# q for four batches at once with two levels of seven products, k and v for all batches first

## The chip, the cores and the metric

The kernel runs on one core of a Trainium2 chip. Time is device microseconds of one execution. TensorE (PE) multiplies, VectorE (DVE), ScalarE (ACT) and GpSimd (POOL) work on elements, SyncE (SP) issues nearly all transfers. PE writes to PSUM, eight banks of 128 partitions x 512 f32 columns; DVE and ACT read PSUM, POOL reads only SBUF. All data are f32.

## The reference

One pre-norm block over x of 8 batches x 256 tokens x 512. Cut to what matters:

```python
x = x + attention(layernorm(x), w_qkv, w_o)
x = x + ffn(layernorm(x), weight, bias, centroids, assignments)

# attention: 32 heads, 8 key heads (kv), head size 128, G = 4 query heads per key head
q, k, v = split(h @ w_qkv)                       # w_qkv: 512 x (4096 + 1024 + 1024)
scores = q @ k.T / sqrt(128) - slope[head] * sqrt(distance), masked to the past
out = softmax(scores) @ v
out @ w_o                                        # 4096 x 512

# ffn: p = softmax(h @ centroids.T / 0.1) over 64 clusters; hits = p > 0.01
# h @ weight.T + bias, kept where the row has a hit and the column's cluster has one anywhere
```

The factor on the bias and the draw of x don't change the work.

## The kernel before

The kernel is written for a scheduler that keeps the order of the program: each engine executes its instructions as the Python code emits them, and waits only for data and for buffers. The order of the code is the schedule.

**Tiling.** Two batches (512 tokens) make a pair `p`; a pair and a key head make a group `g` (32 of them), and a group has two units, one per batch (`u`, 64 of them). Unit `u` computes the scores of four query heads against one key head over 256 tokens. The causal mask is cut into quarters of 64 tokens (`Q`), so that only 1280 of 2048 columns of scores are made: `scores` streams 2 x 384 columns and four small late blocks, which lie in two halves of the array.

**Seven products for eight.** `strassen` (line 146) splits each of the projections of q, k and v once into 2 x 2 blocks and forms the result from seven block products instead of eight, with sums of blocks as factors (`a_sums`, `b_sums`, lines 117 and 130). Products 1, 6, 7 and 4 add up in one PSUM bank, which ACT copies out after each of them; products 2 and 5, 3 sit in other banks, and DVE adds them to the copies. `project_out` (line 505) does the same with the output projection of one unit. A q product of a group is four matmuls of 256 columns (line 155), so a group has 28.

The sums of the weights are made anew for every pair: POOL makes those of w_q (`a_sums(gp, wq[g + 2], ...)`) and of w_o and w_k, DVE those of w_v and of x. k and v of a pair are projected between the units of the pair (`project_k`, `project_v`), those of the next pair ahead of it.

**One unit in the order of the loop** (line 724 on). `scores(u)`; `attend(u - 2, 0)`; POOL's late adds of the output (`flush_adds`, line 548) and `subtract_max(u - 1)`; then, between steps of q, k and v (`qq`, `e`): the maximum of unit u over keys (`over_keys`, line 412), the attention `av` of unit u - 2, the exps of u - 1, the FFN tile of that slot (`f`), the output projection of u - 2 (`w`), the sums over keys of u - 1 (`sum_old`) and `rows()`.

`rows` calls `over_quadrants` (line 426): PE transposes the row statistics, DVE reduces them and takes a reciprocal, SP stores 64 x 32 numbers to HBM and loads them back as a broadcast to 128 partitions, once for the maximum (line 450) and once for 1 / sum (line 448). POOL subtracts that maximum in the next unit (line 457), ACT takes the exp, DVE sums it, and the next `rows` needs this sum.

**Around the loop.** x is normalised by pairs and transposed on PE (`norm_tile`). The alibi bias is made once for each key head in the first pair, kept in HBM and reloaded. The FFN of a pair runs during the next pair; the last two pairs' tiles run at the end. After the loop the column selection is known and the output rows are chosen and stored.

Of the kernel before, what the change touches and what calls it, by code (L numbers as in the profile page):

```python
# [14 lines left out]
F32 = mybir.dt.float32  # L15
# [9 lines left out]
NCL = 64  # L25
P = 128
NC_H = H // P
PT_TOK = 2 * S
NPAIR = B // 2
TPP = PT_TOK // P  # L30
NT = B * S // P
EPS = 1e-5
# [3 lines left out]
X2_BUFS = 8  # L36
Q = P // 2
DQ = 5 * Q
# [7 lines left out]
def sqrt_distances():  # L46

    r = np.arange(P // 2)  # L50
    quarter = lambda *n: np.concatenate([r + i * (P // 2) for i in n])

    def block(k, q):
        k, q = k[:, None], q[None, :]
        return np.where(q >= k, np.sqrt(np.maximum(q - k, 0).astype(np.float32)), np.float32(MASKED))

    own = block(r, r)
    d = np.concatenate([block(quarter(0, 1), quarter(1, 3, 2)), np.concatenate([own, own]),
                        block(quarter(3, 2), quarter(3))], axis=1)
    return np.ascontiguousarray(d.astype(np.float32))  # L60


@with_exitstack
def block_kernel(
# [3 lines left out]
    w_qkv: bass.AP,  # L68
# [3 lines left out]
    centroids_t: bass.AP,  # L72
# [11 lines left out]
    wpool = ctx.enter_context(tc.tile_pool(name="w", bufs=1))  # L84
    work = ctx.enter_context(tc.tile_pool(name="work", bufs=1))
    small = ctx.enter_context(tc.tile_pool(name="small", bufs=4))
    dram = ctx.enter_context(tc.tile_pool(name="dram", bufs=4, space=bass.MemoryType.DRAM))
    p_acc = ctx.enter_context(tc.tile_pool(name="p_acc", bufs=3, space=PSUM))
    p_long = ctx.enter_context(tc.tile_pool(name="p_long", bufs=1, space=PSUM))
    p_sc = ctx.enter_context(tc.tile_pool(name="p_sc", bufs=2, space=PSUM))  # L90
    p_tp = ctx.enter_context(tc.tile_pool(name="p_tp", bufs=1, space=PSUM))


    x2_hbm = [dram.tile([PT_TOK, H], F32, tag=f"x2_hbm{p}", name=f"x2_hbm{p}", bufs=1) for p in range(NPAIR - 2)]
    y_hbm = [dram.tile([PT_TOK, H], F32, tag=f"y_hbm{p}", name=f"y_hbm{p}", bufs=1) for p in range(NPAIR - 2)]
    alibi_hbm = [dram.tile([P, G * DQ], F32, tag=f"al_hbm{kv}", name=f"al_hbm{kv}", bufs=1) for kv in range(NKV)]

    sub = ALU.subtract
    gp, ve = nc.gpsimd.tensor_tensor, nc.vector.tensor_tensor

    def a_side(raw, s1, s2, s4):

        return dict(A11=raw[0], A12=raw[1], A21=raw[2], A22=raw[3], S1=s1, S2=s2, S3=raw[2], S4=s4)

    def b_side(raw, t1, t2, t4):

        return dict(B11=raw[0], B12=raw[1], B21=raw[2], B22=raw[3], T1=t1, T2=t2, T3=raw[1], T4=t4)

    def a_sums(tt, a, which="S1 S2 S3 S4"):
        for s in which.split():
            if callable(a[s]):
                a[s] = a[s]()  # L120
            if s == "S1":
                tt(a["S1"], a["A21"], a["A22"], ALU.add)  # L122
            elif s == "S2":
                tt(a["S2"], a["S1"], a["A11"], sub)  # L124
            elif s == "S3":
                tt(a["S3"], a["A11"], a["A21"], sub)
            else:
                tt(a["S4"], a["A12"], a["S2"], sub)

    def b_sums(tt, b, which="T1 T2 T3 T4"):  # L130
        for s in which.split():
            if callable(b[s]):
                b[s] = b[s]()
            if s == "T1":
                tt(b["T1"], b["B12"], b["B11"], sub)
            elif s == "T2":
                tt(b["T2"], b["B22"], b["T1"], sub)
            elif s == "T3":
                tt(b["T3"], b["B22"], b["B12"], sub)
            else:  # L140
                tt(b["T4"], b["B21"], b["T2"], sub)
# [4 lines left out]
    def strassen(name, tag, a, b, pairs, c, n):  # L146
# [14 lines left out]
        def step(i):  # L161
            if i in (1, "5p") or i == 5 and 5 not in ps:
# [3 lines left out]
                if at == 5:  # L166
                    product(5, ps[5], True)
# [917 lines left out]
```

## Time and profile before

| what | value |
|---|---|
| median of 3 runs | 1392.85 us (1392.62 to 1394.12) |
| profiled execution, first to last instruction | 1390.6 us |
| what lies around it in the median run | 2.25 us |
| PE busy, matmuls recorded | 1379.6 us (99%), 6391 |
| DVE busy | 934.6 us (67%) |
| POOL busy | 957.5 us (69%) |
| ACT busy | 379.7 us (27%) |
| mean granted TensorE clock | 0.999 |
| transfers | 194.54 MB, mean 140 GB/s |

How to read it: busy time is a union over an engine's instructions and says nothing by itself of what the end waits for. Matmuls are pipelined, and their recorded lengths overlap, so what one costs is read from the chain of waits, where each row holds only the time up to the next. A row of a group gives line, engine, operation, tiles written and read, shapes and count, then busy time and mean ns of one, then the engine's idle time before it and who ended it.

### The profile page before, as it was taken

How to read it: one execution, taken by the hardware profiler on the slowest of the kernel's cores; microseconds unless marked ns; L12 is line 12 of the kernel's file. 1: busy time of each engine (PE TensorE's matmuls, PEld its weight loads, DVE VectorE, ACT ScalarE, POOL GpSimd, SP SyncE). 2: the span in 40 equal slices, each digit the busy share in tenths (PEclk: the TensorE clock that was granted, in tenths of full speed). 3: DMA queues.
4: the chain of work that ended last, by engine and by line, in shares of the span. 5: the costliest groups of instructions: out<-in, count | busy, mean ns of one | idle time of the engine just before them, and what ended most of it. 6: DMA issues, size and time to landing. Idle time of an engine off the chain costs nothing.

```text
span 1390.6 us, 18165 instructions
## 1 busy us (share of the span) xinstructions
PE 1379.6 (99%) x6391; PEld 1082.7 (78%) x6391; DVE 934.6 (67%) x1852; ACT 379.7 (27%) x776; POOL 957.5 (69%) x1049
## 2 busy tenths in 40 slices
PE   9999999999999999999999999999999999999998
PEld 7777877877877778777878787877787778778775
DVE  5567756786556665768666767576766686666876
ACT  3322223422232212332213322233222122212332
POOL 6477757787575765768757577576867777577673
PEclk9999999999999999999999999999999999999999
DMA  5436343344242544423334435354414352424344
GB/s 200 138 98 206 108 151 130 138 156 141 95 175 80 183 162 150 168 101 142 118 123 146 132 131 186 125 171 156 141 61 156 111 194 103 156 87 149 138 154 137
DMA packets 88041, 194.54 MB, mean 140 GB/s; under 512 B 11824, under 2 KB 20784, under 8 KB 87952
## 3 DMA queue, kind: packets, MB, share of 16 engines
q1 hardware_dynamic: 86800, 191.52, 39.7%
q10 hardware_dynamic: 1104, 1.70, 0.5%
q8 instruction: 52, 0.85, 0.2%
q14 instruction: 37, 0.30, 0.1%
q0 software_dynamic: 48, 0.16, 0.0%
HBM read 179.21 MB, written 14.16 MB: 139 GB/s over the span
## 4 chain that ended last, share of the span: by engine, by line
PE 92%; DVE 5%; DMA 1%; POOL 1%; issue 1%; ACT 0%; SPq 0%; DVEq 0%; POOLq 0%; ACTq 0%
PE ps_oa L519 15%; PE ps_qa L155 15%; PE av L478 10%; PE ps_qc L155 8%; PE ps_oc L519 7%; PE sc L401 6%; PE sc_late L408 4%; PE ps_va L155 4%; PE ps_ka L155 4%; PE ps_ob L519 4%; PE ps_qb L155 3%; PE ps_f L565 2%; PE ps_kc L155 2%; PE ps_vc L155 2%; PE ps_lg L565 2%; PE ps_vb L155 1%
## 5 line engine op out<-in xcount | busy, mean ns | idle before, releaser
L551 POOL TENSOR_TENSOR x<-x,snap 128x256 f32<-128x256 f32 x189 | 136.5, 739 | 198.0 <-DVE x L545 134.6
L457 POOL TENSOR_TENSOR s<-s,bc 128x768 f32<-128x768 f32 x64 | 116.6, 1822 | 135.1 <-DMA bc<-row_hbm 135.1
L415 DVE TRANSPOSE_TENSOR_REDUCE r<-s 128x40 f32<-128x1280 f32 x128 | 192.6, 1505 | 10.2 <-ACT s L823 7.3
L478 PE MATMUL av<-s,v 64*128 64x256 f32 (+2 forms) x640 | 170.8, 442 | 0.0
L171 ACT COPY qT<-ps_qa 128x512 f32<-128x512 f32 x128 | 74.8, 584 | 320.5 <-PE ps_qa L155 320.5
L534 ACT COPY snap<-ps_oa 128x256 f32<-128x256 f32 x189 | 70.4, 373 | 271.8 <-PE ps_oa L519 271.8
L478 PEld LDWEIGHTS av<-s,v 128*128 128x128 f32 (+1 forms) x640 | 91.3, 188 | 61.8 <-issue 55.8
L519 PE MATMUL ps_oa<-wo,oT 128*128 128x256 f32 x512 | 132.2, 381 | 0.8 <-DVE oT L500 0.8
L155 PE MATMUL ps_qa<-xT,wq 128*128 128x256 f32 x512 | 124.2, 385 | 0.0
L155 PEld LDWEIGHTS ps_qa<-xT,wq 128*128 128x128 f32 x512 | 94.4, 190 | 21.8 <-issue 10.2
L519 PEld LDWEIGHTS ps_oa<-wo,oT 128*128 128x128 f32 x512 | 91.8, 190 | 17.5 <-DVE oT L500 2.4
L462 POOL TENSOR_TENSOR s<-s,bc 64x256 f32<-64x256 f32 (+1 forms) x128 | 96.8, 757 | 9.8
L401 PE MATMUL sc<-qT,kT 128*128 128x384 f32 x256 | 93.1, 486 | 0.0
L421 DVE TENSOR_TENSOR r<-r 64x8 f32<-64x8 f32 x128 | 82.2, 642 | 1.7
L403 DVE SCALAR_TENSOR_TENSOR s<-sc,alibi 128x384 f32<-128x384 f32 x128 | 69.7, 555 | 18.0 <-PE sc L401 14.0
L545 DVE TENSOR_TENSOR x<-x,ps_oc 128x256 f32<-128x256 f32 x128 | 53.4, 418 | 28.3 <-PE ps_oc L519 27.4
L122 POOL TENSOR_TENSOR o_s<-oT 128x256 f32<-128x256 f32 x64 | 48.1, 752 | 34.3 <-DVE oT L495 34.1
L408 PE MATMUL sc_late<-qT,kT 128*64 128x256 f32 x512 | 69.4, 392 | 0.0
L420 DVE TENSOR_TENSOR r<-r 128x8 f32<-128x8 f32 x128 | 65.2, 509 | 4.4
L519 PE MATMUL ps_oa<-wo_t,o_s 128*128 128x256 f32 x256 | 65.8, 379 | 0.7 <-POOL o_s L124 0.7
L495 DVE TENSOR_TENSOR oT<-av,bc 128x512 f32<-128x512 f32 x64 | 44.2, 690 | 32.9 <-DMA bc<-row_hbm 17.6
L519 PE MATMUL ps_oa<-wo_t,oT 128*128 128x256 f32 x256 | 65.8, 379 | 0.0
(207 smaller groups left out, 2952.1 us busy)
## 6 DMA issues: line engine op xcount, KB each, us to landing
bc<-row_hbm SPq DMA_DIRECT2D x128, 512.0 KB, 4.9
wq<-in_w_qkv SPq DMA_DIRECT2D x32, 1024.0 KB, 7.8
wo<-in_w_o SPq DMA_DIRECT2D x32, 1024.0 KB, 8.0
alibi<-al_hbm SPq DMA_DIRECT2D x24, 640.0 KB, 8.8
wv<-in_w_qkv SPq DMA_DIRECT2D x8, 1024.0 KB, 11.5
wk<-in_w_qkv SPq DMA_DIRECT2D x15, 512.0 KB, 9.7
al_hbm<-alibi SPq DMA_DIRECT2D x8, 640.0 KB, 9.0
x<-in_x SPq DMA_DIRECT2D x16, 256.0 KB, 9.6
```

Source lines behind the costliest of these rows:

```text
L155: nc.tensor.matmul(bank[:, cols], lhsT=lhsT, rhs=rhs, start=first and j == 0, stop=j == len(mms) - 1, skip_group_check=True)
L171: nc.scalar.copy(x, like(ps[1], x))
L401: nc.tensor.matmul(sc, lhsT=kT[:, quarters(t0, 0, 2)], rhs=qT[:, 2 * i : 2 * i + 2, quarters(t0, 1, 3)], start=True, stop=True)
L408: nc.tensor.matmul(sc[ts(half, Q), ts(k // 2, G * Q)], lhsT=kT[:, quarters(t0, key, 1)], rhs=qT[:, :, quarters(t0, query, 1)], start=k < 2 ...
L415: nc.vector.tensor_reduce(a, s.rearrange("p (j q) -> p j q", q=32), AX.X, op, apply_transpose=True)
L421: nc.vector.tensor_tensor(first[Q:, :, 2 * QT :], first[Q:, :, 2 * QT :], heads(own[Q:]), op)
L457: gp(s[:, :AT_E], s[:, :AT_E], mx[:, :AT_E], sub)
L462: gp(x, x, mx_of(quarter)[own], sub)
L478: mm = lambda out, lhsT, rhs, start, stop: nc.tensor.matmul(out, lhsT=lhsT, rhs=rhs, start=start, stop=stop, skip_group_check=True)
L519: nc.tensor.matmul(bank[:, :HH], lhsT=x[:, e, :], rhs=y[:, e, :], start=first and e == 0, stop=e == 1, skip_group_check=True)
L534: nc.scalar.copy(snap[:, j], ps[1][:, :HH])
L551: gp(c, c, s, ALU.add)
```

## The change

Nearly the whole program is rewritten; the reference, the masks and the tail keep their form.

**Four batches at once, two levels.** A group is now half of the batches (4 x 256 tokens) and one key head: 16 groups of four units. q of a group is a product of 512 x 512 by 512 x 1024, cut into 4 x 4 blocks of 128 rows (256 tokens): the seven products are applied to 2 x 2 outer blocks, and inside each outer product again, 49 matmuls of 256 columns for 64.

```diff
+class Factors:          # 4 raw outer blocks, 3 outer sums, and 3 inner sums for each of the 7
+    def of(self, outer, inner):
+        o, j = self.role[outer], self.role[inner]
+        return self.group(o, o + 1)[:, 0, j] if j < 4 else self.i[:, o, j - 4]
...
+    class Blocks:
+        def product(self, bank, col, outer, inner, first):
+            w, x = self.a.of(outer, inner), self.b.of(outer, inner)
...
+                mm(bank[:, col : col + S], w, x, first, True)
...
+        def outer(self, o, chain, pair):
...
+            def snap(i, j):
+                to, x = self.sub_of(c, i, j), self.like(ps["c"], 0)
+                if o == 7:
+                    add_to(to, x)
+                else:
+                    nc.scalar.copy(to, x)
...
+                elif i == 7:
+                    self.product(ps["c"], 0, o, 7, False)
+                    snap(1, 1)
...
+                        add_to(self.pair_of(c), ps["p"].rearrange("p (t c) -> p t c", t=2))
...
+                elif i == 3:
+                    self.product(ps["p"], S, o, 3, False)
+                    add_to(self.sub_of(c, 0, 1), self.like(ps["p"], S))
+                    self.finish(o)
```

Inner products 1, 6, 7 and 4 add up in one bank (`chain`), copied by ACT after each; 2, 5 and 3 share a bank (`pair`), added by DVE. `finish` queues the outer merges, adds of 128 x 1024, six per group; in the loop POOL makes them (`background`), DVE what is left at a group's end (`by_vector`).

**Sums of factors are made once.** In the first phase POOL makes the three outer and 21 inner sums of w_q for each key head (`fq`), SP stores all 49 blocks to HBM (`keep`) and loads the raw weights of the next head into that buffer (`load_stage`). In the loop the 49 blocks are loaded in 14 pieces per group (`reload_wq`). x's 49 blocks of the second four batches are stored too (`x1_end`) and loaded over the first four's in groups 6 and 7 (`x_reload`).

```diff
+    def fq(kv, parts=(0, 1, 2), tt=gp):
+        f = stage_of(kv)
+        for i in parts:
+            if i == 0:
+                outer_sums(tt, f, (1, 2, 3, 4), True)
+            else:
+                inner_sums(tt, f, *((0, 4), (4, 7))[i - 1], True)
+
+    def keep(kv):
+        f, dst = stage_of(kv), fq_hbm[kv]
+        nc.sync.dma_start(dst[:, : 16 * P]..., f.raw)
+        nc.sync.dma_start(dst[:, 16 * P : 28 * P]..., f.s)
+        nc.sync.dma_start(dst[:, 28 * P :]..., f.i)
```

**k and v of all batches in a first phase,** with one level of seven products and matmuls of 512 columns (`One`, `job_v`, `job_k`: 14 matmuls each, eight jobs of k and eight of v), two jobs woven step by step. Each job's result is stored to HBM (`flush_outs`); unit u + 2's k and v, 128 KB each, are loaded at the end of unit u (`load_kv`). x of the second four batches is normalised and transposed on PE; x of the first four is handed in transposed, and DVE applies the norm with a broadcast of its statistics (`scale0`). The order of the phase:

```diff
+    run(woven(v1[0], v1[1], STEPS[2:]), {
...
+        8: [L(roots0, 6), L(fq, 1)], 9: [spread0]})
+    flush_outs()
+    run(woven(v1[2], v1[3], STEPS[2:]), {
+        3: [L(keep, 2), L(load_stage, 4)], 6: [L(scale0, ve, 0, 0, 0), L(scale0, ve, 0, 0, 1)],
+        8: [L(scale0, ve, 0, 1, 0), L(scale0, ve, 0, 1, 1), L(fq, 4)]})
...
+    run(woven(v0[0], v0[1]), {1: [L(outer_sums, ve, X0, (1, 2), False)], 3: [L(outer_sums, ve, X0, (3, 4), False)], 4: [L(fq, 3)], 8: [L(keep, 4), L(load_stage, 6), L(sums_k, 0)], 13: [L(keep, 3), L(load_stage, 5)]})
+    run(woven(v0[2], v0[3]), {0: [L(fq, 6)], 1: [flush_outs], 4: [L(load_raw, FK[1], w_k[1], 0, 1, 3, 2), L(inner_sums, ve, X1, 0, 4, False, (1, 2, 4))],
+                              9: [L(sums_k, 1), L(fq, 5), L(keep, 6), L(load_stage, 0)]})
...
+    run(woven(*k1[0]), {1: [flush_outs], 2: [L(keep, 5), L(load_stage, 7)], 3: [L(fq, 0)],
+                        10: [L(inner_sums, ve, X1, 4, 7, False, (1, 2, 4))]})
+    run(woven(*k1[1]), {0: [L(fq, 7)], 1: [flush_outs]})
...
+    run(woven(*k0[0]), {1: [flush_outs, L(keep, 7)], 4: [x1_end], ...
```

The last quarter of k (`k0[1]`) runs between the 49 products of the first group's q.

**The unit.** The columns of scores are laid out anew (512 + 256 + late), the maximum is subtracted in two pieces, the late adds of the output are one add of 128 x 1024. The folding of row statistics uses reduces instead of adds, the sum over keys three transposing reduces instead of one, and the maximum comes back in five broadcasts:

```diff
+        if has_max:
+            nc.sync.dma_start(mx("b"), flat(16, 32).partition_broadcast(P))
+            nc.sync.dma_start(mx("rest"), flat(16, 24).partition_broadcast(P))
+            nc.sync.dma_start(mx("own", slice(0, Q)), flat(0, 8).partition_broadcast(Q))
+            nc.sync.dma_start(mx("own", slice(Q, P)), flat(24, 32).partition_broadcast(Q))
+            nc.sync.dma_start(mx("q1"), flat(8, 16).partition_broadcast(P))
+        if has_sum:
+            nc.sync.dma_start(inv_sb, flat(J0, 2 * J0).partition_broadcast(P))
```

The steps of q for the next group stand at fixed places of a unit, at most 14 per unit (`z()` takes the next one where SPOTS has a 1):

```diff
+    SPOTS = ((1, 0) + (1,) * 12,) * 3 + ((1, 0, 1, 1, 1, 1, 0, 0, 1, 1, 0, 0, 0, 0),)
+    def q_counts(g):
+        return (14, 21, 7, 7) if g == 0 else (14, 14, 14, 7)
...
+        elif u < NU - 1:
+            z(), av(0), exp_old(0), z(), exp_old(1), av(1), z(), sum_old(), background(7.0), f(0), rows_max()
+            w(1), z(), f(1), f(1.5), w(2), z(), z(), f(2), norm(0), w(6), rows(), z()
...
+            z(), norm(1), z()
+            w(7), z(), background(5.0), f(3), norm(2), w(3), z(), norm(3), w(4), q(99)
```

The alibi bias is computed by ACT once per group instead of being reloaded. FFN tiles run in units 35, 39, 43, 47, 51, 60, 61 and 62, the other eight after the loop. The weights and x are handed in in another order. All buffers are regions of one SBUF tile that is laid out by hand (`region`, `place`).

## The prediction

> **What bounds the kernel now.** I read the page first, then the chain of waits in order of time, then the groups by form, and last the timeline of one unit and the transfers by stretch. The page's first line and the shares of the chain:
>
> ```profile
> span 1390.6 us, 18165 instructions
> ...
> PE 1379.6 (99%) x6391; PEld 1082.7 (78%) x6391; DVE 934.6 (67%) x1852; ACT 379.7 (27%) x776; POOL 957.5 (69%) x1049
> ...
> PE 92%; DVE 5%; DMA 1%; POOL 1%; issue 1%; ACT 0%; SPq 0%; DVEq 0%; POOLq 0%; ACTq 0%
> ```
>
> The chain in order of time shows what a matmul costs where PE is the bound (start, length, what):
>
> ```profile
> 703.06 1.29 PE sc L401 x4
> 704.35 1.01 PE sc_late L408 x8
> 705.37 0.63 PE av L478 x4
> ...
> 707.06 1.73 PE ps_qa L155 x8
> ...
> 710.51 1.29 PE av L478 x4
> ```
>
> Eight records of 256 columns take 1.73 us, 0.216 each. An f32 matmul leaves two records (q calls 32 groups x 28 = 896 matmuls, and its groups hold 1792), so one of 256 columns costs 0.431 us. The last row is one matmul of 512 and one of 256 columns: 1.29 - 0.43 = 0.86 for 512, no cheaper per column. Counted this way: q 896 x 0.431 = 386, the output projection as many, k and v 224 each = 97 + 97, scores 64 x 2.30 = 147, attention 64 x 2.35 = 150, the FFN 62, transposes 21: 1347 of the 1391 us. The rest is 6.5 us before the first transpose of x, 5 after the last matmul, and under 1 us of gaps in most stretches of 50 us. So the kernel is bound by columns streamed through PE, and an edit that removes columns pays in full if nothing else comes late.
>
> **What the change takes off PE.** q: 16 groups of four batches, 49 products each, 784 matmuls instead of 896: 112 x 0.431 = 48.3 us. k and v: 224 matmuls of 512 columns for 448 of 256, some 0.8 us. x of the first four batches is also handed in transposed, so 16 tiles become 8 and 32 transposes go: 128 of them are some 14 us, so 3.5. Scores (512 + 256 + late columns for 2 x 384 + late), attention, output projection and FFN stream the same columns. Together 52.6 us: 1390.6 - 52.6 = 1338.0, if every wait stays as it is.
>
> **What it adds on the other engines, per unit.** A unit is one batch of one key head; 64 of them. Without k and v its PE time is scores 2.30 + attention 2.35 + output 6.03 + the small transpose 0.11 = 10.8, plus 14, 14, 14 and 7 q products: 16.8 in the first three units of a group, 13.8 in the fourth, 16.1 on average against some 20 before. The others must now fit there. The rows:
>
> ```profile
> L551 POOL TENSOR_TENSOR x<-x,snap 128x256 f32<-128x256 f32 x189 | 136.5, 739 | 198.0 <-DVE x L545 134.6
> L457 POOL TENSOR_TENSOR s<-s,bc 128x768 f32<-128x768 f32 x64 | 116.6, 1822 | 135.1 <-DMA bc<-row_hbm 135.1
> L415 DVE TRANSPOSE_TENSOR_REDUCE r<-s 128x40 f32<-128x1280 f32 x128 | 192.6, 1505 | 10.2 <-ACT s L823 7.3
> L421 DVE TENSOR_TENSOR r<-r 64x8 f32<-64x8 f32 x128 | 82.2, 642 | 1.7
> ```
>
> POOL: 256 columns 0.74, 768 columns 1.82, so 0.54 per 256 more, 1024 columns 2.36. Per unit: subtracting the maximum 768 + 512 columns 3.10 (was 4.07 in four pieces), sums of the attention output 4 x 0.74 = 2.96, late adds as one of 1024 columns 2.36, w_o's sums 4 x 1.27 / 4 = 1.27, q's six merges of 1024 columns per group 14.2 / 4 = 3.54. Sum 13.2 of 16.1; the sums of w_q leave the unit. Before: 957.5 / 64 = 15.0 of 20.
>
> DVE: scores 1.80 as now; maximum 1.505 plus two short reduces, a copy and a memset, some 0.5; sum the same columns in three pieces, 1.9 + 0.5; rows 0.90; attention 2 x 0.69; output 0.69 + 0.42; q per group 7 x (0.69 + 0.42) and four of 0.42 more, 9.4 / 4 = 2.36. Sum 12.0, 75% of the unit. The short reduces are in no row: below, L434's 0.28 for 32 x 128; above, L421's 0.64. I take 0.2 to 0.3, since L421 is mostly waiting: in its timeline single ones take 0.17, others 1.2, beside POOL. The Trainium skill (SBUF — State Buffer, Who interferes with whom) says that a DVE instruction with two SBUF inputs and a POOL instruction that reads SBUF lock each other out for a whole instruction, and that a reduce never does. L421 agrees with that; by the rule two waits per row statistic vanish, but in the first phase the DVE sums of x meet a POOL that hardly rests.
>
> ACT: exps 0.85 + 0.63, output copies 4 x 0.37, q copies 24 x 0.37 / 4 = 2.2, the bias computed anew: 5.6 of 16.1. Hidden, as long as no copy of q stands behind an exp that waits for POOL, since q's next product adds onto the bank that is copied.
>
> SP and the transfers: what used to be made in the unit is now loaded, k and v with 0.26 MB per unit, q's factors with 14 transfers and 3.2 MB per group, w_o 1.05 as now, broadcasts 1.15 per unit. That is 2.5 MB per unit, 155 GB/s against a mean of 140 now. They are issued when a unit's PE work ends, at most 2.6 MB at once, 7.5 us at 348 GB/s; the next row store comes 11 us later. Hidden; if the row store met them, it would cost up to those 7.5 us in two units of four.
>
> **The row loop.** The maximum of a unit goes through PE, DVE, SP, HBM and back; then POOL, ACT, DVE and the next transpose. One turn now (start, length):
>
> ```profile
> 700.20 0.27 PE L430 MATMUL tp_r<-ident,r 128*64 128x128 f32 x1
> ...
> 701.49 0.45 SPq L438 DMA_DIRECT2D row_hbm<-row  x1
> ...
> 703.28 0.33 SPq L450 DMA_DIRECT2D bc<-row_hbm  x1
> 703.65 0.43 SPq L448 DMA_DIRECT2D bc<-row_hbm  x1
> ...
> 707.30 1.81 POOL L457 TENSOR_TENSOR s<-s,bc 128x768 f32<-128x768 f32 x1 [3.09 <-DMA bc<-row_hbm]
> ```
>
> 7.1 us from the transpose to the subtraction. The change makes the one broadcast of the maximum five (four wait issues of some 0.4 on SP, and 1.15 MB for 1.05), and puts the broadcast of 1/sum sixth. The first subtraction needs two of them: 7.5. Then 3.1 on POOL, 0.63 for the last exp, 2.4 of sums on DVE behind up to 1.1 of other work, 0.3: 14 to 15 us, against 16.1 of PE, 15.9 into the short fourth unit and 15.1 out of it. The sixth broadcast, some 10 us after the transpose, is 4 to 5 us into the next unit, where DVE first needs it; waiting there, DVE holds up q's adds and through their banks PE. So the loop fits by about 1 us. I charge 0.1 us per unit for lateness, 6 us; bounds 0 and 0.6 (36).
>
> At a group's end the last q product is followed by only four output products (3.4 us), while a DVE add (0.42, behind 1.3 of rows) and a POOL merge of 2.36 must pass before the next scores: 15 x 0.4 = 6 us; bounds 0 and 15.
>
> **The first phase.** 224 matmuls of 512 columns, 193 us, and 8.6 at the start as now; q of the first group runs beside the last quarter. POOL makes all sums of w_q here: per head 4 + 4 of 512 and 4 of 384 columns, some 14.2 us, 113 for eight, with v's and k's sums 133. The transfers are the risk: read 20 MB (x, x transposed, weights, a broadcast), write 49 MB (eight sets of factors 25.7, k and v 16.8, x's factors 6.4): 69 MB in some 226 us, 305 GB/s. What the queue can do (last two numbers: share of the DMA engines, GB/s):
>
> ```profile
> 5.00:10.00 5.00, 4.00 (x34) 3.16 (x32) 3.29 (x13) 2.75 (x6) 1.16 (x3) 1.00 1.01 348
> ...
> 15.00:20.00 5.00, 5.00 (x24) 4.25 (x23) 3.40 (x4) 0.96 (x2) 4.85 (x5) 1.00 1.05 389
> ```
>
> At 348, 198 us of transfers: 88% of the phase. The Trainium skill (DMA: Bandwidth & Descriptors, Specifications) puts the limit from HBM at about 358 GB/s per core; by that it would be 193 us, against the change all the same. SP issues in order, and each head's factors must be finished before their store is issued, so the stores of v stand behind POOL. Following the order by hand, k's first job wants, at 115 us, a buffer that v's third pair of jobs left, and its store lands near 118: one stall of some 3 us, with 2 more where x's sums come late. I take 5; bounds 0, and 45 at 250 GB/s.
>
> From there to the third unit the loop has no cover: the last merge of the first q (1.3 to 2.4), the first maximum (unit 0 is 8 us long, its turn 14): 8 us; bounds 2 and 20. At the end, four units without q, three with an FFN tile (4.3), 15.1 us against the same loop, and one without: 6 us more than now; bounds -4 and 15.
>
> **Sum.** 1338.0 + 6 + 6 + 5 + 8 + 6 = 1369. The median of the runs is 2.3 us above the profiled span: 1371 us.
>
> **Rivals.** (1) All of it hides: 1338 + 2 + some 6 = 1346. For it: PE's queue holds q products between all steps. (2) Slower: the row loop becomes the clock of the units. Price: 60 us for each us by which it passes PE's 16.1; beyond about 0.5 us per unit the 52.6 are gone. At 17.0 us: 1371 - 6 + 54 = 1419. For it: five broadcasts, and a DVE at 75% with waits in its queue; against it: POOL now waits 135 us for the broadcast without any cost. (3) The first phase runs at the pace of transfers and POOL: at 250 GB/s 276 us for 226, less what is in the sum, 1371 + 45 = 1416; from about 275 GB/s it decides the sign. That the saving isn't there at all I leave out: the products can be counted.
>
> **How the numbers follow.** Forecast 0.46 (1356 to 1386), all hidden 0.17 (1342 to 1356), row loop 0.20 and first phase 0.17 (1386 to 1440). Of the last two, 0.02 is faster all the same and 0.04 the same. A measurement of this kernel can tell about 0.2%, 2.8 us. Faster: 0.46 + 0.17 + 0.02 = 0.65; same 0.04; slower 0.31. The range leaves out some 0.05 below and 0.1 above: 1345 to 1425.
>
> **What would show it.** Right: PE's records fall by 224 for q, 448 for k and v and 32 transposes; chain PE about 90%; PE near 9 in all slices but a few before 230 us; granted clock unchanged. Row loop: PE waiting for DVE before the small transpose or before the output products in every unit, POOL waiting for the broadcast 3 us and more. First phase: slices before 230 us with PE under 9 and DMA at 9, ACT copies of k or v waiting for a DMA. I would be wrong if the units' PE time were not 16 us, or if POOL's merges made the q steps wait.

## The result, and the profile after

The changed kernel takes 1501.8 us (median of 4 runs, 1500.0 to 1503.0) against 1392.9 us for the kernel before: 1.078 times as long, 95% interval 1.076 to 1.079. I had said 1371 us, 1345 to 1425, with 0.65 on faster. The sign was wrong, and the time lies 77 us above the range.

The head of the page of the changed kernel and the shares of its chain:

```profile
span 1498.2 us, 17918 instructions
...
PE 1386.3 (93%) x5672; PEld 947.4 (63%) x5672; DVE 1005.8 (67%) x2074; ACT 455.6 (30%) x1023; POOL 974.5 (65%) x731
...
PE 65%; DVE 22%; DMA 4%; POOL 3%; issue 3%; SPq 1%; ACT 1%; POOLq 0%; DVEq 0%; ACTq 0%
```

PE has 719 records fewer (I had counted 704: 224, 448 and 32), and yet it is busy for longer than before (1379.6). A record's end is modelled, so busy time holds some of the waiting. The chain is plainer: PE had 92% of it, now 65%; DVE went from 5% to 22%. DVE's own busy time rose by 71 us, though q, k and v are cheaper now.

I measured what PE loses in another way: from the start of one PE record to the start of the next, less what such a record takes back to back (0.2156 us for 256 columns, 0.4295 for 512, and so on). Summed by stretch, in us (the middle stretch runs from the fifth to the 59th of the small row transposes, one for each unit):

| kernel | first 100 us | from there to the 5th row transpose | 54 units | rest | sum |
|---|---|---|---|---|---|
| before | 5.3 | 0.1 | 17.5 | 5.7 | 28.6 |
| after | 26.3 | 34.0 | 92.9 | 37.0 | 190.2 |

What is left is work. Before: 1390.6 - 28.6 - 6.1 (ahead of the first and behind the last matmul) = 1355.9. After: 1498.2 - 190.2 - 5.6 = 1302.4. So the change does save 53.5 us of matmul time, where I had counted 52.6; and it loses 161.6 us to waits and gaps, where I had charged 31 (6 + 6 + 5 + 8 + 6). The difference, 108 us, is the result.

The same stretches in the windows view (length, then busy time of PE, PEld, DVE, ACT and POOL, PE's granted clock with 1.00 as full speed, the DMA engines' share, GB/s):

```profile
0.00:100.00 100.00, 83.56 (x209) 38.55 (x209) 64.87 (x98) 21.97 (x44) 59.37 (x49) 0.95 0.66 252
100.00:240.00 140.00, 139.85 (x358) 67.30 (x357) 50.72 (x63) 30.68 (x59) 87.88 (x71) 1.00 0.85 325
240.00:339.00 99.00, 78.66 (x311) 53.01 (x310) 55.64 (x119) 26.27 (x62) 50.79 (x35) 0.88 0.47 155
339.00:1323.00 984.00, 936.48 (x4187) 685.61 (x4186) 720.51 (x1502) 315.25 (x744) 698.99 (x515) 1.00 0.47 152
```

The second row is the first phase, which I had feared: 325 GB/s, DMA engines 85% busy, and PE without a gap. The rows around it, with the clock at 0.95 and 0.88, are the start and the way into the loop.

In the units, the row transposes stand 18.2, 18.2, 18.3 and 16.0 us apart; I had counted 16.1 on average. The chain in order of time through one unit (start, length, what):

```profile
571.86 8.81 PE ps_b L188 x42
...
580.68 0.70 DVE arena L707
...
581.41 1.52 DVE r L712
...
582.96 0.17 DVE r L724
...
583.14 0.17 DVE r L726
...
583.34 1.57 DVE r L727
...
584.95 0.07 DVE r L728
...
585.05 0.70 DVE arena L794
...
585.80 4.15 PE ps_b L188 x18
589.95 0.11 PE ps_b L733
590.06 8.80 PE ps_b L188 x42
```

No broadcast and no POOL instruction stands in it. PE finishes the late scores at 580.7. Then DVE, in the order of its queue, adds their bias (L707), takes the unit's maximum (L712 and the short instructions behind it) and only then does the attention multiply (L794) that the first output product needs: 5.1 us. PE has 4.4 us of q and attention work to put beside that, and waits 0.7 us here; 39 such waits for L794 add up to 32.8 us. Over the units from 330 to 1320 us the broadcasts hold 1.7% of the chain. One instruction in this row is out of proportion, the copy of 64 x 8 elements at L727. The groups by form (busy us, mean ns of one):

```profile
L862 POOL TENSOR_TENSOR arena<-arena 128x1024 f32<-128x1024 f32 x62 | 146.4, 2361 | 2.0 <-DVE arena L856 1.0 <-ACT arena L844 1.0
...
L727 DVE COPY r<-r 64x8 f32<-64x8 f32 x128 | 111.5, 871 | 4.0
...
L726 DVE TENSOR_REDUCE r<-r 64x8 f32<-64x16 f32 x128 | 21.4, 167 | 2.9
L724 DVE TENSOR_REDUCE r<-r 128x8 f32<-128x16 f32 x128 | 19.0, 148 | 2.2
```

The copy takes five times as long as a reduce over twice as many elements. In the unit above it ends at 584.89, with POOL's late add of 1024 columns (L862, right behind the subtraction of the maximum), which ends at 584.87 (timeline):

```profile
582.50 2.37 POOL L862 TENSOR_TENSOR arena<-arena 128x1024 f32<-128x1024 f32 x1
...
583.34 1.55 DVE L727 COPY r<-r 64x8 f32<-64x8 f32 x1
```

### The profile page after: what moved, and what is told of

It reads as the page before. It is cut to its first block, busy times and chain, and to the rows that moved or that the text cites. A ratio compares the mean times of both kernels' runs of the same rounds, so it can differ in the third digit from the quotient of the medians.

```text
span 1498.2 us, 17918 instructions
## 1 busy us (share of the span) xinstructions
PE 1386.3 (93%) x5672; PEld 947.4 (63%) x5672; DVE 1005.8 (67%) x2074; ACT 455.6 (30%) x1023; POOL 974.5 (65%) x731
## 4 chain that ended last, share of the span: by engine, by line
PE 65%; DVE 22%; DMA 4%; POOL 3%; issue 3%; SPq 1%; ACT 1%; POOLq 0%; DVEq 0%; ACTq 0%
PE ps_b L188 59%; DVE r L712 6%; DVE r L727 5%; PE ps_b L888 4%; DVE arena L707 3%; DVE arena L794 2%; DMA arena<-row_hbm 2%; DVE arena L243 2%; POOL arena L171 1%; DMA arena<-in_w_v 1%; DMA row_hbm<-row 1%; POOL arena L184 1%; DVE r L726 1%; DVE prob_max L939 1%; DVE r L724 1%
## 5 line engine op out<-in xcount | busy, mean ns | idle before, releaser
L188 PE MATMUL ps_b<-arena 128*128 128x256 f32 (+3 forms) x5216 | 1297.9, 420 | 76.7 <-DVE arena L794 32.8
L188 PEld LDWEIGHTS ps_b<-arena 128*128 128x128 f32 (+2 forms) x5216 | 875.4, 186 | 479.0 <-issue 227.4
L755 POOL TENSOR_TENSOR arena<-arena 128x768 f32<-128x768 f32 (+1 forms) x128 | 195.7, 1546 | 224.6 <-DMA arena<-row_hbm 222.7
L240 ACT COPY arena<-ps_b 128x256 f32<-128x256 f32 x384 | 142.9, 372 | 408.6 <-PE ps_b L188 394.5
L288 POOL TENSOR_TENSOR arena<-arena 128x1024 f32<-128x1024 f32 x90 | 211.7, 2353 | 62.0 <-DVE arena L243 59.6
L777 POOL TENSOR_TENSOR arena<-arena 128x256 f32<-128x256 f32 x256 | 180.7, 727 | 98.7 <-DVE arena L798 93.7
L243 DVE TENSOR_TENSOR arena<-arena,ps_b 128x256 f32<-128x256 f32 (+1 forms) x288 | 150.1, 521 | 137.6 <-ACT arena L240 87.3
L712 DVE TRANSPOSE_TENSOR_REDUCE r<-arena 128x16 f32<-128x512 f32 (+2 forms) x256 | 200.6, 821 | 2.1
L707 DVE SCALAR_TENSOR_TENSOR arena<-ps_b,arena 128x512 f32<-128x512 f32 (+1 forms) x192 | 113.8, 599 | 114.2 <-PE ps_b L188 113.2
L844 ACT COPY arena<-ps_b 128x256 f32<-128x256 f32 x248 | 92.0, 371 | 296.7 <-PE ps_b L188 280.1
L862 POOL TENSOR_TENSOR arena<-arena 128x1024 f32<-128x1024 f32 x62 | 146.4, 2361 | 2.0 <-DVE arena L856 1.0
L727 DVE COPY r<-r 64x8 f32<-64x8 f32 x128 | 111.5, 871 | 4.0
L171 POOL TENSOR_TENSOR arena<-arena 128x512 f32<-128x512 f32 (+1 forms) x44 | 66.0, 1523 | 41.0 <-DMA arena<-in_w_q 26.3
L184 POOL TENSOR_TENSOR arena<-arena 128x512 f32<-128x512 f32 (+1 forms) x64 | 77.7, 1240 | 1.3
L888 PE MATMUL ps_b<-arena 128*128 128x256 f32 (+3 forms) x264 | 70.8, 424 | 1.3 <-ACT arena L884 1.3
L794 DVE TENSOR_TENSOR arena<-ps_b,arena 128x512 f32<-128x512 f32 x64 | 44.1, 690 | 20.0 <-PE ps_b L188 9.6
```

Of the source, the lines that this page charges most:

```text
L184: tt(o, p, q, op)
L188: mm = lambda out, lhsT, rhs, start, stop: nc.tensor.matmul(out, lhsT=lhsT, rhs=rhs, start=start, stop=stop, skip_group_check=True)
L240: nc.scalar.copy(to, x)
L243: ve(to, to, b, add)
L288: tt.append((2.37, lambda tt=gp: tt(q(to), q(to), q(x), add)))
L707: nc.vector.scalar_tensor_tensor(s[:, part], sc, D ** -0.5, bias_sb[:, part], ALU.mult, add)
```

## The experiments

All medians in us; the ratio is to the kernel before. "Units" is the distance of the row transposes in the first three units of a group and the fourth.

| run | time | ratio, 95% interval | units | lost by stretch |
|---|---|---|---|---|
| after | 1501.8 | 1.076 to 1.079 | 18.2, 16.0 | 26.3, 34.0, 92.9, 37.0 |
| e1 reduce for the copy | 1455.6 | 1.042 to 1.046 | 17.3, 15.9 | 25.0, 33.7, 51.8, 37.0 |
| e2 late add first | 1473.1 | 1.055 to 1.058 | 17.3, 16.6 | 24.4, 34.3, 66.3, 39.5 |
| e3 two broadcasts | 1488.1 | 1.065 to 1.070 | 17.3 to 18.9, 17.2 | 23.9, 35.8, 73.0, 41.2 |
| e4 start and unit 2 | 1489.9 | 1.065 to 1.069 | 18.2, 16.0 | 22.3, 27.6, 92.6, 40.3 |
| e5 = e1, scores together | 1455.4 | 1.043 to 1.046 | 17.3, 15.9 | 23.4, 34.6, 50.3, 35.6 |
| e6 = e1 and e3 | 1467.1 | 1.050 to 1.054 | 17.3, 17.3 | 26.4, 36.1, 57.2, 40.0 |
| e7 = e1, 1/sum third | 1508.8 | 1.081 to 1.085 | 17.4 to 19.2, 17.5 | 21.8, 41.1, 94.5, 42.9 |
| e8 = all of e1, e4, e7 | 1492.2 | 1.067 to 1.073 | 17.4 to 18.6, 17.4 | 22.2, 23.6, 85.6, 43.7 |
| e9 = e8 without e7's order | 1442.7 | 1.033 to 1.038 | 17.3, 15.9 | 23.1, 22.7, 49.4, 37.6 |
| e10 = e1, late scores by attention | 1448.8 | 1.037 to 1.042 | 17.1, 15.9 | 25.0, 34.7, 46.8, 35.5 |
| e11 late add in four | 1465.4 | 1.049 to 1.053 | 17.3, 16.4 | 25.3, 34.8, 58.3, 39.2 |
| e12 = e9, e10 and the end | 1438.3 | 1.032 to 1.035 | 17.1, 16.0 | 22.2, 23.8, 42.5, 39.2 |
| e13 = e1, work left out | 1432.3 | 1.022 to 1.033 | 17.3, 15.9 | 10.2, 33.0, 51.0, 26.3 |

The first 100 us lose 21.8 to 26.4 in the nine kernels that leave them as they are, so that differences under some 4 us there say nothing.

**e1: a reduce in the place of the copy.**

```diff
-        nc.vector.tensor_copy(r[:Q, at + 24 : at + 32], r[:Q, q2 : q2 + 8])
+        nc.vector.tensor_reduce(r[:Q, at + 24 : at + 32], r[:Q, q2 : q2 + 8].unsqueeze(2), AX.X, op)
```

> One line of the row statistics: DVE's copy of eight columns becomes a reduce over a unit dimension, same values. Theory A (lock): the units run at the row loop's 18.2 us because this copy (128 times, mean 871 ns, 111 us in all) and the attention multiply queued behind it stand locked beside POOL's late add of 1024 columns. Then the reduce takes 0.15 to 0.2 us, the row transposes stand 16.4 to 17.2 us apart in full units instead of 18.2, and the kernel takes 1420 to 1460 us instead of 1502. Theory B (broadcasts): five broadcasts set the loop; DVE's copy only fills time in which DVE would wait anyway; distance 18.0 or more and a time above 1490 us. Theory C (two-input operations): the attention multiply is locked out by the same late add in the copy's place; the copy becomes short, the multiply longer, and the time falls by less than 25 us.

46 us less. The group, and the chain through a unit (by form, then in order of time):

```profile
L727 DVE TENSOR_REDUCE r<-r 64x8 f32<-64x8 f32 x128 | 19.6, 153 | 4.0
```

```profile
405.85 0.11 PE ps_b L733
405.96 17.14 PE ps_b L188 x78
423.10 0.11 PE ps_b L733
```

In this unit the chain is PE alone. The same eight columns take 0.153 us instead of 0.871, DVE is 84 us less busy in all (921.6), and of the 75 us that the units lose more than before, 41 are gone. Full units take 17.3 us, a little more than expected. The gain is theory A's. But what A shared with my prediction, that the row loop through the broadcast is the clock at 18.2, is not what the chain of the changed kernel shows: what the lock (DVE's copy held up by POOL's instruction; e2 and e11 test it) lengthened was the row of DVE instructions between the late scores and the attention multiply.

The Trainium skill (SBUF — State Buffer, Who interferes with whom) names copies among the DVE operations that can take the port pair shared with GpSimd, for a whole instruction, and says of reduces that they never do; 0.871 against 0.153 us agrees. Its condition for that mode (VectorE: DVE Perf Modes, What auto-detection actually checks) is one source and the destination in SBUF, with outermost lengths that are even (or equal); eight columns meet it. In which mode the copy ran no view here shows.

**e2: the late add ahead of the subtraction.** POOL waits there for the broadcast anyway.

```diff
+        flush_adds()
         if 1 < u < NU:
             subtract_max(u - 1, 0), subtract_max(u - 1, 1)
-        flush_adds()
```

> POOL's late add of 1024 columns is issued ahead of the subtraction of the maximum, where POOL waits for the broadcast, not behind it; the copy stays. Theory A: nothing long on POOL follows the subtraction, so copy and attention multiply start at once; distance of the row transposes 16.4 to 17.4 us, time 1425 to 1470 us; the subtraction starts at most 0.5 us later. Theory B: no gain, the subtraction starts when the broadcast lands; 1490 us or more. If the late add itself comes late (it waits for ACT's copy of the last output product), the subtraction moves back by up to 2.4 us and the kernel gets slower than 1502.

29 us less, 3 us above theory A's range. The copy's mean falls by half:

```profile
L727 DVE COPY r<-r 64x8 f32<-64x8 f32 x128 | 57.7, 451 | 4.0
```

So it is the neighbour that makes the copy long, not the copy. Less is won than in e1: the copy is still three times as long as the reduce, and the fourth unit gets longer (16.6).

**e11: the late add in four pieces of 256 columns,** as the kernel before had it.

```diff
-            gp(c, c, snap, add)
+            for j in range(4):
+                gp(c[:, ts(j, HH)], c[:, ts(j, HH)], snap[:, ts(j, HH)], add)
```

> The changed kernel with its copy, but POOL's late add of 1024 columns (2.36 us) as four of 256 (0.73 us each), as the kernel before had it. Theory A (lock of a whole instruction): the copy waits at most for one of the four, its mean falls from 0.87 to 0.3 to 0.5 us and the attention multiply starts up to 1.3 us earlier: units 17.4 to 17.9 us, time 1465 to 1490. If the copy waits for POOL to be idle and not for one instruction, its mean and the units' 18.2 stay, or get worse by the 0.6 us that four pieces take longer: 1500 us or more.

36 us less, at the lower end of theory A:

```profile
L727 DVE COPY r<-r 64x8 f32<-64x8 f32 x128 | 58.4, 456 | 4.0
```

POOL is busy 26.5 us longer in all (1001.0 for 974.5), and the kernel is faster. The copy waits for the POOL instruction in flight, so the length of one POOL instruction counts here, not POOL's load.

**e3: two broadcasts for five.** The second subtraction takes the maxima of the first one's columns, so that another value is subtracted. The edit does a second thing: the broadcast of 1/sum now comes third.

```diff
-            nc.sync.dma_start(mx("own", slice(0, Q)), flat(0, 8).partition_broadcast(Q))
-            nc.sync.dma_start(mx("own", slice(Q, P)), flat(24, 32).partition_broadcast(Q))
-            nc.sync.dma_start(mx("q1"), flat(8, 16).partition_broadcast(P))
...
-        gp(s_sb(u)[:, part], s_sb(u)[:, part], mx_sb[:, part], sub)
+        gp(s_sb(u)[:, part], s_sb(u)[:, part], mx_sb[:, :n], sub)
```

> Three of the five broadcasts of the maximum (own twice, q1) are left out; the second subtraction takes its maximum from the columns of the first, so that the subtracted maximum is another one there. SP issues three fewer broadcasts, and the one of 1/sum comes third instead of sixth. Theory B (broadcasts set the loop): the second subtraction and all behind it start 1 to 2 us earlier, distance 16.2 to 17.2, time 1400 to 1450. Theory A (lock): the first subtraction waits for the first two broadcasts as before, the late add still stands behind the second and locks the copy; distance 17.8 to 18.2, time 1475 to 1502.

14 us less, in the range of theory A. By itself that doesn't clear the five broadcasts, since the place of 1/sum has a price of its own (e7), which may hide what fewer broadcasts give. That they don't set the changed kernel's units is shown by the chain above and by e1, which leaves all five in place. The copy's mean is 0.63 us here, because POOL and DVE meet at other moments.

**e6: e1 and e3 together.**

> The reduce for the copy and, with it, three of the five broadcasts of the maximum left out (the second subtraction uses the first one's maximum columns, another value). If the row loop without the lock lies below PE's time, as theory A says, the broadcasts no longer set anything in the 55 units with q: unit distance stays 16.8, and only the units near the end without q gain, 3 to 10 us: 1446 to 1453 us. If the five broadcasts still hold the loop at 16.8, the distance falls to 16.3 and the time to 1425 us or less.

Neither: 11.5 us more than e1. **e7** gives the reason, the place of 1/sum; on e1 it only moves the broadcast of 1/sum (512 KB) ahead of the last three of the maximum:

```diff
             nc.sync.dma_start(mx("rest"), flat(16, 24).partition_broadcast(P))
+        if has_sum:
+            nc.sync.dma_start(inv_sb, flat(J0, 2 * J0).partition_broadcast(P))
+        if has_max:
             nc.sync.dma_start(mx("own", slice(0, Q)), flat(0, 8).partition_broadcast(Q))
...
-        if has_sum:
-            nc.sync.dma_start(inv_sb, flat(J0, 2 * J0).partition_broadcast(P))
```

> The reduce for the copy, and the broadcast of 1/sum issued third instead of sixth, ahead of own (twice) and q1. In the units with an FFN tile DVE's attention multiply waits 1.2 to 2.3 us for that broadcast; with it third it lands some 1.5 us earlier. Theory E (sixth broadcast): the waits in the units with an FFN tile and at the end fall, 5 to 10 us less than 1455.6. Rival: the second subtraction, whose broadcasts now come 0.4 us later each, is what those units hang on; then nothing is gained or 2 to 5 us lost.

53 us more than e1, against both expectations. The issues of the broadcasts (KB, median us from issue to landing), of the changed kernel and then of e7:

```profile
arena<-row_hbm SPq DMA_DIRECT2D x64, 512.0 KB, 4.8
...
arena<-row_hbm SPq DMA_DIRECT2D x128, 128.0 KB, 4.2
```

```profile
arena<-row_hbm SPq DMA_DIRECT2D x64, 512.0 KB, 6.5
...
arena<-row_hbm SPq DMA_DIRECT2D x128, 128.0 KB, 5.5
```

Counted from the row store's issue, the first broadcast lands at 5.5 us in the changed kernel and 5.7 in e7, the second at 6.7 and 7.5, the last of the maximum at 7.9 and 10.3 (means over the units; e1, which differs from e7 by this order alone, has 5.5, 6.7 and 7.9 too). The second one is issued at the same time in both; it lands 0.8 us later because 512 KB are issued right behind it. In e3 and e6, where 512 KB stand behind it as well, it lands at 7.6 and 7.7. This is a true row loop. The chain through one unit of e7:

```profile
556.52 0.12 PE ps_b L733
...
557.65 1.67 DMA row_hbm<-row
...
561.87 6.87 DMA arena<-row_hbm
...
568.91 1.26 POOL arena L756
570.16 2.33 POOL arena L863
572.52 0.37 ACT arena L845
572.89 0.28 ACT arena L240
573.22 1.99 PE ps_b L188 x8
575.21 0.11 PE ps_b L733
```

Transpose, row store, broadcast, second subtraction, late add, two copies on ACT, the q products whose bank the copy frees, transpose: 18.7 us. PE waits 36 us for such copies (L240) in e7, 9.6 in e1, and over the units of e7 the broadcasts hold 19.9% of the chain. With this order, two broadcasts (e6) are 42 us faster than five (e7). So the loop that I had priced exists, lies in e1's full units just under PE's 17.3 us, and landings 0.8 to 2.4 us later make it the clock.

**e4: two edits in two stretches.**

```diff
-        norm_write(norm_scale(seen[i]), [xin[1][i]], True)
+        norm_write(norm_scale(seen[i]), [xin[1][i]])
...
-            q(3), top(), q(6), exp_of(0, 0), exp_of(0, 1), q(3), sum_old(), q(4), rows(), q(99)
+            q(3), top(), q(6), exp_of(0, 0), exp_of(0, 1), q(3), sum_old(), q(4), rows(), q(99), background(99)
```

> Two edits that act in two different stretches. (a) The first eight tiles of x are normalised by ACT, not by DVE. If DVE's writes are what POOL's sums of v's factors lock (0.55 us alone, 1.6 to 2.7 us beside them), the stretch up to 100 us loses 8 to 14 of its 26 us of idle PE; if PE's start hangs on the loads or on the clock, 3 us at most. (b) The POOL merges left by q of the first unit run in unit 1, ahead of the subtraction that waits 12 us for its broadcast, not in unit 2 behind it. If they caused the stop of 8.8 us in unit 2, it goes and the units from there on start 6 to 9 us earlier; if the broadcast caused it, it stays. Together 1480 to 1488 us, by the other causes about 1500.

The second edit does what was expected. In the changed kernel four merges of q stood behind the subtraction on POOL (timeline; in brackets the wait ahead of the instruction):

```profile
289.18 3.02 POOL L755 TENSOR_TENSOR arena<-arena 128x768 f32<-128x768 f32 x2 [12.45 <-DMA arena<-row_hbm]
...
292.16 9.49 POOL L288 TENSOR_TENSOR arena<-arena 128x1024 f32<-128x1024 f32 x4
296.94 0.37 ACT L240 COPY arena<-ps_b 128x256 f32<-128x256 f32 x1 [12.44 <-POOL arena L288]
297.37 2.93 PE L188 MATMUL ps_b<-arena 128*128 128x256 f32 x6 [8.55 <-ACT arena L240]
```

PE's stop of 8.8 us becomes 2.4, and the way into the loop loses 6.4 us less; the whole, 1489.9 us, lies 2 us above the range. The first edit is inconclusive: the first 100 us lose 22.3, within what other kernels show without it. DVE's writes were indeed locked there (L382, the same tile size, before and beside POOL's sums of v's factors, which begin at 16.21):

```profile
15.18 0.55 DVE L382 TENSOR_SCALAR arena<-arena,rstd,shift 128x512 f32<-128x512 f32 x1
...
16.62 1.95 DVE L375 SCALAR_TENSOR_TENSOR shift<-mv,rstd 128x1 f32<-128x1 f32 x1
18.61 2.65 DVE L382 TENSOR_SCALAR arena<-arena,rstd,shift 128x512 f32<-128x512 f32 x1
```

but with ACT in their place the chain is hardly shorter: ACT takes 0.8 us per tile, its next square root stands behind a copy of v that waits for PE, and L375 stays on DVE, up to 2.02 us long there.

**e5 and e10: where the q steps stand.** On e1.

```diff
-    SPOTS = ((1, 0) + (1,) * 12,) * 3 + ...
+    SPOTS = ((0, 0, 2) + (1,) * 11,) * 3 + ...      # e5
+    SPOTS = ((1, 0, 0, 2) + (1,) * 10,) * 3 + ...   # e10
```

> On the kernel with the reduce for the copy (1455.6 us, units 16.8 us apart): in three units of four the q step between the first two pieces of the scores is moved behind the third. Theory S (switches): what is left above PE's 16.1 is the some 0.1 us that PE loses wherever 512-column scores stand beside 256-column q products; one such pair of switches fewer per unit takes 0.1 to 0.2 us off, 5 to 9 us in all. Theory D (order for DVE): the q step there gives DVE time to take the first piece out of its bank; without it PE waits for DVE's 0.69 us adds of the bias before it may write the third piece, and the time rises by 5 to 30 us.

No change (1455.4 against 1455.6): neither theory. PE still goes 2 times per unit from 256 to 512 columns, and theory S had nothing to win there: in the changed kernel the last record of 256 columns ahead of one of 512 takes 0.216 us from start to start (median of 106 places), as it does among its own kind, and the first of 512 takes 0.43.

> On the kernel with the reduce for the copy: in three units of four the q step between the late scores and the first attention matmuls is moved behind the attention multiply, so that the two forms that use half of the array stand side by side again, as they did before the change. Theory S (switches): leaving a 64-row form for a q product takes 0.20 us and the way from q to the 64-column form of the attention 0.09; side by side they take 0.15 in all, so 0.14 us per unit in some 42 units goes: 1448 to 1452 us. Theory D (cover): that q step covers DVE's work ahead of the attention multiply, PE then waits there by up to 0.86 us, and the time rises by 5 to 30 us.

6.8 us less, as theory S has it. Full units take 17.1 us instead of 17.3.

**e8, e9, e12: sums of edits.** e8 is e1, e4's second edit, e7's order, the last merges of the first q by DVE, and a start with four tiles written by DVE, four by ACT, each tile's statistics issued ahead of the copies of v's products. e9 is e8 without e7's order. e12 is e9, e10 and, in the units from the 60th on, `rows()` right behind the first output product.

> All edits that should help together: the reduce for the copy (46 us), the merges of the first q run in unit 1 (6 us in the stretch of unit 2), 1/sum broadcast third, the first eight tiles written by DVE for four and by ACT for four, with each tile's statistics issued ahead of the copies of v's products (2 to 8 us in the first 60 us), and the last merges of the first q by DVE (1.2 us) instead of POOL (2.35 us), 2 to 4 us near 250 us. If the causes are separate the sum is 1426 to 1440 us; if the row loop takes back what the other edits give, above 1445. No version of this should come below the 1392.9 us of the kernel before: some 36 us more than before stay in the start, the way into the loop and the end.

> Three edits that act in three stretches: the reduce for the copy, the merges of the first q run in unit 1 (and its last merges by DVE), and the start with the first eight tiles written by DVE for four and by ACT for four. The order of the six broadcasts stays as it was. In the kernel that also moved the broadcast of 1/sum to third place these edits took 10 us off 200 to 300 us and 3 off the first 100. Theory F (broadcast order cost the 53 us there): without that move the units stand at 17.3, 17.3, 17.0 and 15.9 as with the reduce alone, and the time is 1455.6 - 13 = 1439 to 1446 us. Rival: an earlier start only shifts the meeting of POOL's work and the broadcasts, the units go to 17.5 or more, and the time is above 1450.

> The three edits of the sum (1442.7 us), the late scores side by side with the attention (6.8 us less by itself), and a new one at the end: in the three units from the 60th on, which have no q, the row statistics go through PE right after the first output product, not after the FFN tile's products, 5 us after DVE has them ready. Theory G (place): the distances of 18.7 to 19.6 us there come from that place, since the broadcast of 1/sum lands 9.5 us behind the row store and the attention multiply waits for it; placed earlier the distances fall by 1 to 3 us each, and the stretch behind 1300 us loses 4 to 9 of its 33 us of idle PE. Rival: those units hang on DVE's work for the FFN tile, which would now stand behind the row statistics; then nothing is gained there. In all 1426 to 1433 us by G, 1434 to 1438 by the rival; still above 1393.

e8 came out above 1445, as its rival says, and by far more than it says; e9 came out where it was expected: 49.5 us between them for the place of one broadcast. e12 is the best version found, 3.3% slower than the kernel before. Its stretch at the end loses no less than e9's (39.2 and 37.6): theory G fell. With 1438.3 us it stands at the upper end of the rival's range.

**e13: work left out at both ends.** On e1: the first eight tiles are transposed as loaded, and the last four units take no new maximum.

```diff
     def look(i):
-        seen[i] = norm_root(norm_stats(xin[1][i]))
+        pass
...
     def prepare(i):
-        norm_write(norm_scale(seen[i]), [xin[1][i]], True)
+        pass
...
-                over_quadrants(u, r, own and not alone, True)
+                over_quadrants(u, r, own and not alone and u < 60, True)
```

> The kernel with the reduce for the copy, with work left out in two stretches that are read apart. (a) The first eight tiles of x are transposed as loaded, their statistics and normalisation left out. Of the 25 us that PE loses up to 100 us: if the chain of statistics, root, scale and write per tile sets the pace, 10 us or less stay; if the loads of x and v's weights, the transposes' copies or POOL's sums of v's factors do, 16 or more stay. (b) The units from the 60th on take no new maximum: its rows and broadcasts are left out there, and the subtraction uses the values that lie in place. Of the 37 us that PE loses from the 60th unit on: if the row loop sets those units, 20 to 25 stay and their distances fall from 18.7 and 19.6 to 16 to 17 us; if the FFN tiles' chain through DVE and ACT does, 33 or more stay.

(a) 10.2 us stay of 25.0: the chain of statistics, root, scale and write costs the start 15 us. Part of these is the clock: in e1 eleven records of 512 columns in the first 100 us came 0.85 us apart instead of 0.43, in e13 none did. (b) 26.3 stay of 37.0, between the two expectations: the maxima cost 10.7 of the 31 us that the end loses more than before. What costs the other 20 is not settled; the largest single wait left there, 2.9 us, is that of the FFN's transposes for ACT's normalisation behind the last units.

## Why the prediction was wrong, point by point

**Columns: right.** 53.5 us of matmul time for 52.6.

**First phase: right in the part I doubted.** Over the first 240 us the transfers ran at 295 GB/s (252 in the first 100, 325 behind them) for an estimate of 305, and PE had no gap between 100 and 240 us; neither POOL nor the transfers set that stretch. The limit of 358 GB/s that the prediction quotes stands beside its own row of 389; the measurement decides.

**The units: the step that failed.** I charged 6 us for the row loop and 6 for group ends; the units lose 75 us more than before. Of that, 41 are the lock (e1). Two errors lie in the term "maximum 1.505 plus two short reduces, a copy and a memset, some 0.5". Its size: for the maximum the copy alone takes 1.28 us on average (trace of the changed kernel, 64 of them), up to 2.34, so that the 0.5 became 1.67 (0.15 + 0.17 + 1.28 + 0.07). I had the rule for two-input operations in hand, wrote that two waits per row statistic vanish since reduces come in their place, and did not ask the same of the copy that came with them. Its place: I added DVE's work to 12.0 us of 16.1 and called it hidden. DVE's share came out right (720.5 of 984 us, 73%, for 75%) because unit and work both grew: 13.3 us of 18.2 per unit for 12.0 of 16.1; without the lock it is 11.9 (e1). But the load was not the question. From the end of the late scores through the attention multiply, 3.7 us of DVE instructions, without the lock, meet 4.4 us of PE work; with it they are 5.1, and that doesn't fit, whatever the load.

Counted by waits of over 0.25 us each, the units (320 to 1290 us) have 57 us after, 21 in e1, and 2 before (100 to 1280 us). The 21 left in e1 are spread over several engines and not explained. The rest is many small gaps, most of them out of and into the forms that use half of the array, 0.09 to 0.20 us each. There are 53.5 us of these, and 35.5 before. (This count sets the half-array forms at the pace of full streaming, so its sums, 110.5 and 37.5, stand some 20 us above the table's in both kernels; the difference, 73, agrees with the table's 75.) Part of the 18 us more comes from q steps that now stand between forms that stood side by side: e10 gives 5 us of it back. I had carried before's gaps over and charged nothing for new ones.

**Rival 2 showed its signs, but not its mechanism.** I said that PE would wait for DVE ahead of the output products in every unit and that POOL would wait 3 us and more for the broadcast. Both are in the profile (39 waits for L794, 32.8 us; 3.5 us of POOL's waiting per unit). But the chain of the full units doesn't pass through the broadcast, and e1, with all five in place, brings those units to PE's pace. The loop itself was sized well: 7.9 us to the first subtraction for 7.5 (mean of 54), subtractions 3.05 for 3.1. "Fits by about 1 us" was about right too: in e7 0.8 to 2.4 us more latency make it the clock and cost 53 us. The fear for the sixth broadcast pointed the wrong way: of the two places tried, last is the better by 53 us.

**Start: mis-sized.** "8.6 at the start as now" holds for two tiles of x and the products that follow them. Now eight tiles pass one after another through load, statistics, normalisation, transpose and copy before v's sums can be made, with few products between them. 21 us more are lost, where the whole first phase had 5; 15 hang on the normalisation (e13).

**Way into the loop: 8 charged, 34 lost** (bounds 2 and 20). I had the first maximum and the last merge, not the merges that are issued behind a subtraction that waits 12.5 us (6 us, e4). Another 5 came back in e9, which also lets DVE make the last merges of the first q. The other 23 are not settled.

**End: 6 charged, 31 lost** (bounds -4 and 15). The row loop, which I had named, explains 11 (e13).

Added up, the experiments account for 46 of the 75 us in the units (e1, e10), 15 of the 21 at the start, 11 of the 34 on the way into the loop and 11 of the 31 at the end: half of the 162. What makes up the other half is open. Had the lock and the stop in unit 2 been absent, the kernel would still have been slower than before: e9 stands at 1442.7. The forecast failed by several terms, and as far as the runs explain them they are of one kind: a stretch in which PE has too little work to cover someone's wait.

## What to carry to other kernels

When PE's work is cut, add up for each hand-over what stands in the queue of the engine that releases it, and what PE has to do meanwhile; a load of 75% hides nothing if 5.1 us of it stand in one row against 4.4 us of cover. Beside a busy POOL, look at every small DVE instruction in such a row: here a copy of eight columns cost what POOL's instruction in flight had left, and a reduce over a unit dimension did the same work in 0.15 us. In a group of broadcasts, try issuing last the one that is needed last, above all when it is the largest: here its place was worth 50 us.

## What the runs showed of the hardware that I had not expected

- A 64 x 8 copy took up to 2.34 us beside POOL's 2.36 us add, 0.16 alone; a 128 x 1 operation of two SBUF inputs (L375) 1.95 us, 0.16 alone.
- A transfer issued later delays one issued earlier: 128 KB landed 0.8 us later with 512 KB issued right behind them (e7 against e1), though their own issue had not moved.
- Where PE had waited for some us, PE's records of 512 columns came 0.85 us apart instead of 0.43 for a while, and the granted clock fell to 0.88 in the stretch from 240 to 339 us. Behind the stop at 288 us six records of 256 columns took 2.93 us (the row in e4) instead of 1.29. Records at half pace make up some 18 of the changed kernel's 190 us (8 in the first 100, 5 on the way into the loop, 5 at the end), and under 3 before: a stop cost more than its length here.
